# One gathered tile in 72 fetched row by row from SP's queue: a graph layer on one core

## The chip, the core and the metric

The kernel runs on one core of a Trainium2 chip. A core has TensorE (PE in the profile), VectorE (DVE), ScalarE (ACT), GpSimd (POOL) and SyncE (SP), each with its own instruction stream. They meet through semaphores and share 16 DMA engines. SP computes nothing: it waits, loads registers and issues transfers. POOL issues the indirect transfers, whose row addresses come from a list of indices in on-chip memory. The metric is the device time of one execution in microseconds (us).

## What is computed

A message-passing layer on a graph with 12,500 nodes and 412,500 edges, sorted by target node, 96 channels wide. Cut to what matters:

```python
def _mlp(h, W, b, gamma, beta):
    h = relu(h @ W + b)
    mu, var = mean(h, axis=0), mean(square(h - mean(h, axis=0)), axis=0)
    return gamma * (h - mu) * rsqrt(var + 1e-5) + beta

node_feat = _mlp(x, W_node, b_node, g_node, beta_node)
edge_feat = _mlp(edge_attr, W_edge, b_edge, g_edge, beta_edge)
message = concatenate([x[src], x[dst], edge_feat], axis=1)      # 412500 x 288
message = _mlp(message, W_msg, b_msg, g_msg, beta_msg)
agg = segment_sum(message, dst, num_segments=12500)
return layernorm(x + agg + node_feat)
```

The sources `src` are random, so each of the 412,500 edges needs some row of 96 floats (384 bytes).

## The kernel before

**Tables.** The product of x with the source part and with the target part of `W_msg` is made once per node and kept in device memory: `p_tab` for sources, `q_tab` for targets. An edge then needs the row `p_tab[src]`.

**Tiles, groups, blocks.** A tile is 128 edges, one on each partition; there are 3223. Four tiles (`GT`) make a group: 806 groups (`NG`). Four groups (`BG`) make a block: 202 blocks. `gather(g, pg)` (L162) fetches one group into the buffer `pg` with four indirect transfers issued by POOL (L166), one for each tile: 128 rows of 384 bytes each.

**Early and late groups.** The first 104 groups (`SPILL`) are gathered while the tables, the node part and the edge statistics are computed, and are written out to `spill`. All later groups go into a ring of 21 buffers (`RING`): 21 groups are gathered ahead of the main loop (L355), and from then on one more group is asked for, by `ahead_of` (L332), each time the loop has used one late group (L536 to L538). So group `ahead` goes into the buffer that group `ahead - 21` has just left.

**The main loop** (L514 to L538) goes over `steps`, all groups in the order of `order`: 176 late blocks, with the 26 early blocks spread between them. Its order is written out by hand for all five engines (`manual_schedule`): each engine carries out its instructions in program order. At the first group of block number `s`, SP issues `load(s + 2)` and `fetch(s + 1)`. `load` (L390) fetches edge attributes and relative targets for two blocks at a time (L399, L400), loads one register with the block's first node (L403), and copies target rows from `q_tab` into one of three `rhs` buffers (L408); the address comes from that register. That last transfer waits until PE has done its products (L455) with the `rhs` buffer's former contents. `fetch` (L411) brings an early block back from `spill` (L415). PE makes the edge part and adds the target rows (L440, L455), DVE adds the gathered rows (`message`, L466), ACT applies relu (L473), PE sums by target and collects the statistics (L488), DVE adds the sums into `agg` (L501, L502).

**After the loop** the last statistics are made, and the output is normalised and written (L709 to L742).

Transfers issued by SP take eight completion semaphores in turn, and each transfer waits for the one that used its semaphore before, eight transfers back.

Of the kernel before, what the change touches and what calls it, by code (L numbers as in the profile page):

```python
# [11 lines left out]
F32 = mybir.dt.float32  # L12
I32 = mybir.dt.int32
# [3 lines left out]
ET = mybir.EngineType  # L17
# [3 lines left out]
N, C, E, ED = 12500, 96, 412500, 4  # L21
EPS = 1e-5
P = 128
# [3 lines left out]
GT, GE, BG = 4, 512, 4  # L27
NT = -(-E // P)
NG = -(-NT // GT)
NBL = -(-NG // BG)  # L30
NTP, NGP = NBL * BG * GT, NBL * BG
EP = NGP * GE
# [19 lines left out]
SPILL = 26 * BG  # L52
RING = 21
RAW = 3
SKEW = 8
HB, RB = 2, 3
CL, CE = 2, 2
J = 8


# [12 lines left out]
def gnn(ctx, tc, t):  # L73
    nc = tc.nc
    const = ctx.enter_context(tc.tile_pool(name="const", bufs=1))
    dram = ctx.enter_context(tc.tile_pool(name="dram", bufs=1, space=DRAM))
    p_tab = dram.tile([NN, C], F32, name="p_tab")
# [11 lines left out]
    ring = rpool.enter_context(tc.tile_pool(name="ring", bufs=RING))  # L89
# [16 lines left out]
    wide = const.tile([P, P], F32, name="wide")  # L106
# [52 lines left out]
                (nc.scalar if (c // CH + k) % 2 else nc.sync).dma_start(outs[k][:, c:c + CH, :], r[:, :, k, :])  # L159
            yield  # L160

    def gather(g, pg):  # L162
        tab, idx = (t["x"], src_raw) if g < RAW * BG else (p_tab, src)
        for i in range(min(GT, NT - g * GT)):
            k = g * GT + i
            nc.gpsimd.indirect_dma_start(  # L166
                out=pg[:, i, :], out_offset=None, in_=tab[:, :],
                in_offset=bass.IndirectOffsetOnAxis(ap=idx[:, k:k + 1], axis=0))
        return pg
# [107 lines left out]
    def edge_norm():  # L277

        with tc.tile_pool(name="es", bufs=2) as work, tc.tile_pool(name="es1", bufs=1) as one, \
                tc.tile_pool(name="es_ps", bufs=4, space=PSUM) as ps:  # L280
            stats = one.tile([P, NS, NBL, 6], F32, name="estats")
            for b in range(NBL):
                if b % J == 0:
                    yield
                    ea = work.tile([P, J, GE], F32, name="ea")
                    n = min(J, NBL - b)
                    for i in range(NS):
                        nc.sync.dma_start(ea[Q * i:Q * i + 2 * EK, :n, :],
                                          t["ea"][EK * i:EK * (i + 2), b:b + n, :])
                for i in range(NS):  # L290
                    k = NS * b + i
                    if k % 2 == 0:
                        pr = ps.tile([P, 2, GE], F32, name="pr")
                    nc.tensor.matmul(pr[:, k % 2, :], wide[Q * i:Q * i + 2 * EK, :],  # L294
                                     ea[Q * i:Q * i + 2 * EK, b % J, :], start=True, stop=True)
                    if k % 2:
# [32 lines left out]
            nc.vector.tensor_scalar(w_e, w_msg[:, 2, :], a_e, None, op0=OP.mult)  # L329

    def fast(ring):
        def ahead_of(g):  # L332
            return gather(g, ring.tile([P, GT, C], F32, name="pg"))

        with tc.manual_schedule(engines={ET.SP, ET.Pool}):
            nc.sync.dma_start(q_tab[:WM, :], zero[:WM])
# [18 lines left out]
            got = {g: ahead_of(g) for g in range(SPILL, SPILL + RING)}  # L355
# [11 lines left out]
        with tc.tile_pool(name="fix", bufs=1) as fix, tc.tile_pool(name="msg", bufs=2) as work, \  # L367
# [22 lines left out]
            def load(s):  # L390

                b = order[s]
                first = SPILL // BG
                c, o = ((b - first) // CL * CL + first, CL) if b >= first else (b // CE * CE, CE)
                if c not in eas:
                    o = min(o, NBL - c)
                    eas[c] = work.tile([P, o, GE], F32, name="ea" if b >= first else "eae")
                    for i in range(BG):
                        nc.sync.dma_start(eas[c][Q * i:Q * i + EK, :, :], t["ea"][EK * i:EK * (i + 1), c:c + o, :])  # L399
                    nc.sync.dma_start(eas[c][EK:P:Q, :, :], rel_d[:, c * BG * GE:(c + o) * BG * GE]  # L400
                                      .rearrange("o (b g e) -> (o g) b e", g=BG, e=GE))
                ea = eas[c][:, b - c, :]
                _, val = nc.values_load_multi_w_load_instructions(  # L403
                    base[:, b:b + 1], engines=[ET.SP], min_val=0, max_val=N - 1,
                    skip_runtime_bounds_check_because="they are nodes' numbers")
                rows = q_tab[bass.ds(val[0], WN), :]
                rows = bass.AP(rows.tensor, rows.offset, [[C, WN], [WS * C, BG], [1, C]], None, rows.runtime_checks)
                nc.sync.dma_start(rhs[C:C + WN, s % RB, :, :], rows)  # L408
                block[s] = ea

            def fetch(s):  # L411
                b = order[s]
                if b * BG < SPILL:
                    back = work.tile([P, BG, GT, C], F32, name="pb")
                    nc.sync.dma_start(back, spill[b].rearrange("p g (a c) -> p g a c", a=GT))  # L415
                    for i in range(BG):
                        got[b * BG + i] = back[:, i, :, :]
# [18 lines left out]
            def edges(s):  # L436

                prs[s] = ps.tile([P, BG, GE], F32, name="pr", bufs=1)
                for i in range(min(BG, NG - order[s] * BG)):
                    nc.tensor.matmul(prs[s][:C + WN, i, :], we[Q * i:Q * i + EK + 1, :],  # L440
                                     block[s][Q * i:Q * i + EK + 1, :], start=True, stop=True)

            def prepare(s):

                n = min(BG, NG - order[s] * BG)
                pr, x = prs[s], left[s % 2]
                nc.scalar.activation(x[:C, :n, :], pr[:C, :n, :], AF.Relu)  # L447
                nc.vector.tensor_scalar(x[C:C + WN, :n, :], pr[C:C + WN, :n, :], 0.0, None, op0=OP.is_equal)  # L448

            def linear(k):  # L450
                s, g = steps[k]
                n = min(GT, NT - g * GT)
                zs[k] = zb[k % 2][:, :GT * C].rearrange("p (t c) -> p t c", c=C)
                for i in range(n):
                    nc.tensor.matmul(zs[k][:, i, :], left[s % 2][:KR, g % BG, i * P:(i + 1) * P],  # L455
                                     rhs[:KR, s % RB, g % BG, :], start=True, stop=True)

            def message(k):
                s, g = steps[k]
                n = min(GT, NT - g * GT)  # L460
                i = g % BG
                h, z, pg = hb[s % HB], zs.pop(k), got.pop(g)
                if i == 0:
                    four[0] = work.tile([P, BG, GT, C], F32, name="hs")
                hs = four[0]
                nc.vector.tensor_add(hs[:, i, :n, :], z[:, :n, :], pg[:, :n, :])  # L466
                if i == min(2, NG - 1 - (g - i)):
                    b = g - i
                    nc.vector.tensor_tensor(  # L469
                        h[:, :, :, C + 1:C + 1 + WN], rel[:, b:b + BG, :].unsqueeze(3).to_broadcast([P, BG, GT, WN]),  # L470
                        nodes_of.unsqueeze(2).to_broadcast([P, BG, GT, WN]), op=OP.is_equal)
                if i == BG - 1 and n == GT:
                    nc.scalar.activation(h[:, :, :, :C], hs, AF.Relu)  # L473
                elif i == BG - 1 or g == NG - 1:
                    for o in range(i + 1):
                        m = GT if o < i else n
                        nc.scalar.activation(h[:, o, :m, :C], hs[:, o, :m, :], AF.Relu)  # L477
# [13 lines left out]
            def add(s):  # L491
# [9 lines left out]
                    nc.vector.tensor_tensor(to, pa[:, i:n:2, C + 1:C + 1 + WN], to, op=OP.add)  # L501
                nc.vector.tensor_add(gram[:, :n, :], pa[:, :n, :C + 1], gram[:, :n, :])  # L502

            n, ahead = len(steps), SPILL + RING
            with tc.manual_schedule(engines={ET.SP, ET.Pool, ET.PE, ET.DVE, ET.Activation}):
                load(0)
                fetch(0)
                load(1)  # L510
                edges(0)
                prepare(0)
                linear(0)
                for k in range(n + SKEW):  # L514
                    s, g = steps[min(k, n - 1)]
                    if k < n and g % BG == 0:
                        if s + 2 < len(order):
                            load(s + 2)
                        if s + 1 < len(order):
                            fetch(s + 1)  # L520
                    if k + 1 < n:
                        linear(k + 1)
                    if k < n:
                        message(k)
                    if 0 <= k - BG < n:
                        sums(k - BG)
                    if k < n and s + 1 < len(order):
                        if g % BG == 0:
                            edges(s + 1)
                        if g % BG == 2:  # L530
                            prepare(s + 1)
                        if g % BG == 3 and order[s + 1] < RAW:
                            convert(s + 1)
                    if k >= SKEW and (k - SKEW) % BG == 0:
                        add((k - SKEW) // BG)
                    if k < n and g >= SPILL and ahead < NG:  # L536
                        got[ahead] = ahead_of(ahead)
                        ahead += 1  # L538

            d = fix.tile([C, BG, C], F32, name="d")  # L540
            s = fix.tile([C, 3], F32, name="s")
# [9 lines left out]
    def general():  # L551

        with tc.tile_pool(name="gd", bufs=1, space=DRAM) as gd, tc.tile_pool(name="gfix", bufs=1) as fix, \
# [138 lines left out]
            for b in range(NB):  # L692
# [7 lines left out]
                nc.vector.tensor_copy(agg[:, WM + b * P:WM + (b + 1) * P], px)  # L700

    fast(ring)
    rpool.close()
    bad = nc.values_load(flag, min_val=0, max_val=1, skip_runtime_bounds_check_because="a comparison's result")
# [72 lines left out]
```

## Time and profile before

| | |
|---|---|
| median of 3 runs | 4132.85 us (4130.39 to 4133.86) |
| the profiled execution | 4122.78 us, span 4121.1 us |
| granted TensorE clock, mean | 0.748 |
| POOL busy | 3066.6 us (74%) |
| PE busy | 2680.6 us (65%) |
| DVE busy | 1710.1 us (41%) |
| ACT busy | 1032.9 us (25%) |
| packets of the hardware queue q1 | 69888, 8.4% of 16 engines' time |
| packets of the software queue q0 | 103136, 16.3% of 16 engines' time |

Busy time is what an engine spent in instructions, of the span of one profiled execution. Register, branch, semaphore and DMA-issuing instructions are not counted as busy, so SP does not stand in that list; its instructions show in the views by line, in the timeline and among the waits. The indirect transfers count as busy on POOL. In a group's row, the idle time behind the bar is that of the engine just before those instructions.

### The profile page before, as it was taken

The page shows a single profiled execution, that of the slowest core. Times are in us where ns is not written, and L with a number is a line of the kernel's source. Part 1 is how long each engine was busy: PE and PEld are TensorE (multiplying, and loading weights), DVE is VectorE, ACT ScalarE, POOL GpSimd, SP SyncE. Part 2 cuts the span into 40 slices and gives each one's busy share as a digit, 9 for nine tenths or more (in the row PEclk, how much of TensorE's full clock was granted, in tenths as well). Part 3 has the DMA queues.
Part 4 walks back from the last instruction along what each step waited for, and adds up shares of the span by engine and source line. Part 5 has one row for each costly group of instructions (what it writes and reads, how often), then busy time and mean ns, then how long its engine had stood idle before and what let it go on. Part 6 is the DMA issues. An engine that isn't in the chain of part 4 may idle for free. (4 is left out here: it accounts for less than half of the span.)

```text
span 4121.1 us, 46085 instructions
## 1 busy us (share of the span) xinstructions
PE 2680.6 (65%) x16509; PEld 2234.5 (54%) x16509; DVE 1710.1 (41%) x2609; ACT 1032.9 (25%) x800; POOL 3066.6 (74%) x3244
## 2 busy tenths in 40 slices
PE   4699968866566655666665656665666666665666
PEld 4555536755555555555555545554556555554556
DVE  2599984433333332333233333332333333332333
ACT  1377742221112211122111111211121111111121
POOL 6777777777777777777777777777777777777774
PEclk7555557877778877778787777887777778877786
DMA  8555532222221222122212121222212212222123
GB/s 247 159 109 112 106 72 58 55 54 53 53 53 46 53 54 53 46 54 53 52 47 54 52 54 45 54 54 53 54 45 53 53 46 54 54 52 53 46 53 109
DMA packets 188576, 270.79 MB, mean 66 GB/s; under 512 B 121095, under 2 KB 121480, under 8 KB 187330
## 3 DMA queue, kind: packets, MB, share of 16 engines
q0 software_dynamic: 103136, 158.62, 16.3%
q1 hardware_dynamic: 69888, 95.64, 8.4%
q10 hardware_dynamic: 15312, 13.47, 1.2%
q8 instruction: 133, 2.18, 0.2%
q14 instruction: 107, 0.88, 0.1%
HBM read 225.90 MB, written 41.60 MB: 65 GB/s over the span
## 5 line engine op out<-in xcount | busy, mean ns | idle before, releaser
L166 POOL DMA_INDIRECT pg<-p_tab,src x2807 | 2648.5, 944 | 855.5 <-issue 699.4
L455 PE MATMUL z<-rhs,left 128*128 128x96 f32 x6446 | 1104.7, 327 | 1264.1 <-DVE left L448 1081.2
L455 PEld LDWEIGHTS z<-rhs,left 128*128 128x128 f32 x6446 | 998.7, 236 | 1494.1 <-DVE left L448 1129.8
L466 DVE TENSOR_TENSOR hs<-z,pg 128x384 f32<-128x384 f32 x702 | 391.3, 557 | 1996.5 <-DMA pg<-p_tab,src 1830.9
L488 PE MATMUL pa<-h 128*97 128x128 f32 x6446 | 1006.6, 308 | 4.5 <-DVE agg L501 4.1
L488 PEld LDWEIGHTS pa<-h 128*97 128x97 f32 x6446 | 894.5, 194 | 4.9 <-ACT h L477 4.2
L473 ACT ACTIVATE h<-hs 128x1536 f32<-128x1536 f32 x201 | 298.2, 1483 | 1811.9 <-DVE hs L466 1811.9
L447 ACT ACTIVATE left<-pr 96x2048 f32<-96x2048 f32 x202 | 377.4, 1868 | 914.3 <-PE pr L440 914.3
L448 DVE TENSOR_SCALAR left<-pr 31x2048 f32<-31x2048 f32 x202 | 462.9, 2291 | 21.6 <-ACT left L447 15.3
L166 POOL DMA_INDIRECT stage<-p_tab,src x368 | 353.5, 961 | 124.6 <-issue 107.6
L294 PE MATMUL pr<-ea,wide 10*128 10x512 f32 x1212 | 372.2, 1062 | 21.2 <-DMA ea<-in_ea 21.2
L300 DVE BATCH_NORM_STATS2 estats<-r 128x6 f32<-128x512 f32 x606 | 361.4, 680 | 28.9 <-ACT r L298 28.8
L298 ACT ACTIVATE r<-pr 128x1024 f32<-128x1024 f32 x303 | 293.3, 1024 | 144.2 <-PE pr L294 117.5
L294 PEld LDWEIGHTS pr<-ea,wide 10*128 10x128 f32 x1212 | 209.4, 318 | 182.7 <-issue 87.9
L440 PE MATMUL pr<-ea,we 6*127 6x512 f32 x1404 | 203.4, 648 | 12.3 <-DMA ea<-rel_d 12.3
L469 DVE TENSOR_TENSOR h<-rel,z 128x496 f32<-128x496 f32 x202 | 133.2, 660 | 0.0
L501 DVE TENSOR_TENSOR agg<-pa,agg 97x62 f32 x404 | 89.9, 223 | 63.7 <-PE pa L488 49.1
L502 DVE TENSOR_TENSOR gram<-pa,gram 97x388 f32<-97x388 f32 x202 | 111.3, 551 | 0.2
L466 DVE TENSOR_TENSOR hs<-z,pb 128x384 f32<-128x384 f32 x104 | 57.9, 556 | 108.0 <-PE z L455 107.0
L440 PEld LDWEIGHTS pr<-ea,we 6*127 6x127 f32 x1404 | 55.3, 184 | 38.2 <-issue 13.4
L166 POOL DMA_INDIRECT stage<-in_x,src_raw x48 | 45.5, 947 | 25.1 <-issue 11.0
L266 PE MATMUL py<-center,xp 96*128 96x96 f32 x196 | 42.8, 423 | 26.4 <-ACT xp L261 13.4
(108 smaller groups left out, 566.0 us busy)
## 6 DMA issues: line engine op xcount, KB each, us to landing
pg<-p_tab,src POOLq DMA_INDIRECT x2807
spill<-stage SPq DMA_DIRECT2D x26, 768.0 KB
pb<-spill SPq DMA_DIRECT2D x26, 768.0 KB
ea<-in_ea SPq DMA_DIRECT2D x75, 160.0 KB
rhs<-q_tab SPq DMA_DIRECT2D x202, 46.5 KB
ea<-in_ea SPq DMA_DIRECT2D x352, 20.0 KB
stage<-p_tab,src POOLq DMA_INDIRECT x368
y_d<-y0s SPq DMA_DIRECT2D x12, 384.0 KB
```

Source lines behind the costliest of these rows:

```text
L166: nc.gpsimd.indirect_dma_start(out=pg[:, i, :], out_offset=None, in_=tab[:, :], in_offset=bass.IndirectOffsetOnAxis(ap=idx[:, k:k + 1], ax ...
L294: nc.tensor.matmul(pr[:, k % 2, :], wide[Q * i:Q * i + 2 * EK, :], ea[Q * i:Q * i + 2 * EK, b % J, :], start=True, stop=True)
L298: nc.scalar.activation(r, pr, AF.Relu)
L300: nc.vector.bn_stats(stats[:, (k - o) % NS, (k - o) // NS, :], r[:, 1 - o, :])
L440: nc.tensor.matmul(prs[s][:C + WN, i, :], we[Q * i:Q * i + EK + 1, :], block[s][Q * i:Q * i + EK + 1, :], start=True, stop=True)
L447: nc.scalar.activation(x[:C, :n, :], pr[:C, :n, :], AF.Relu)
L448: nc.vector.tensor_scalar(x[C:C + WN, :n, :], pr[C:C + WN, :n, :], 0.0, None, op0=OP.is_equal)
L455: nc.tensor.matmul(zs[k][:, i, :], left[s % 2][:KR, g % BG, i * P:(i + 1) * P], rhs[:KR, s % RB, g % BG, :], start=True, stop=True)
L466: nc.vector.tensor_add(hs[:, i, :n, :], z[:, :n, :], pg[:, :n, :])
L469: nc.vector.tensor_tensor(h[:, :, :, C + 1:C + 1 + WN], rel[:, b:b + BG, :].unsqueeze(3).to_broadcast([P, BG, GT, WN]), nodes_of.unsqueeze ...
L473: nc.scalar.activation(h[:, :, :, :C], hs, AF.Relu)
L488: nc.tensor.matmul(pas[s][:, g % BG, :C + 1 + WN], h[:r, i, :C + 1], h[:r, i, :C + 1 + WN], start=i == 0, stop=i == n - 1)
```

## The change

In the main loop one tile in 72 is no longer gathered by POOL. The loop counts the groups it asks for in runs of 18 (`SG = SS * ceil(128 / SR)` = 2 * 9). Of the first group of such a run, POOL gathers three tiles, and SP fetches the 128 rows of the fourth by 128 transfers of one row each. They are spread over the run: at every second group SP loads 15 row numbers into 15 registers with one instruction, and issues 15 transfers (8 in the last of the nine portions), each with its address from a register. The row numbers come as a line of 128 integers, fetched into the first row of a constant tile that is not used any more by then (`wide`), once for each run. The first portion waits until the buffer's former group has been used. A run is started so only if it is whole, which gives 37 such runs and 4736 rows.

```diff
+SR, SS = 15, 2
+SG = SS * -(-P // SR)
...
-    def gather(g, pg):
+    def gather(g, pg, without=0):
         tab, idx = (t["x"], src_raw) if g < RAW * BG else (p_tab, src)
-        for i in range(min(GT, NT - g * GT)):
+        for i in range(min(GT, NT - g * GT) - without):
...
+            lin = wide[0:1, :].bitcast(I32)
+
+            def row_numbers(g):
+
+                nc.sync.dma_start(lin, t["rows"][g * GT + GT - 1:g * GT + GT, :])
+
+            def rows_of(pg, lo, hi):
+                _, val = nc.values_load_multi_w_load_instructions(
+                    lin[:, lo:hi], engines=[ET.SP], min_val=0, max_val=N - 1,
+                    skip_runtime_bounds_check_because="they are nodes' numbers")
+                for p in range(lo, hi):
+                    nc.sync.dma_start(pg[p:p + 1, GT - 1, :], p_tab[bass.ds(val[p - lo], 1), :])
...
             n, ahead = len(steps), SPILL + RING
+            row_numbers(ahead)
...
                     if k < n and g >= SPILL and ahead < NG:
-                        got[ahead] = ahead_of(ahead)
+                        m = (ahead - SPILL - RING) % SG
+                        if m == 0:
+                            by_row = ahead if ahead + SG <= NG else None
+                        got[ahead] = ahead_of(ahead, int(ahead == by_row))
+                        if by_row is not None and m % SS == 0:
+                            lo = m // SS * SR
+                            rows_of(got[by_row], lo, min(lo + SR, P))
+                            if m == SG - SS and by_row + 2 * SG <= NG:
+                                row_numbers(by_row + SG)
                         ahead += 1
...
+    give("rows", np.pad(s, (0, EP - E)).reshape(NTP, P))
```

`rows` is the list of sources again, laid out one tile to a line; `ahead_of` passes `without` on to `gather`.

More of the change, by code (lines that the diff above doesn't have):

```diff
@@ L331, in fast, with ahead_of @@
     def fast(ring):
-        def ahead_of(g):
-            return gather(g, ring.tile([P, GT, C], F32, name="pg"))
+        def ahead_of(g, without=0):
+            return gather(g, ring.tile([P, GT, C], F32, name="pg"), without)
         with tc.manual_schedule(engines={ET.SP, ET.Pool}):
```

## The prediction

> **What bounds the kernel now.** First the page's costliest groups: which line owns the span?
>
> ```profile
> L166 POOL DMA_INDIRECT pg<-p_tab,src x2807 | 2648.5, 944 | 855.5 <-issue 699.4
> ...
> L466 DVE TENSOR_TENSOR hs<-z,pg 128x384 f32<-128x384 f32 x702 | 391.3, 557 | 1996.5 <-DMA pg<-p_tab,src 1830.9
> ...
> L166 POOL DMA_INDIRECT stage<-p_tab,src x368 | 353.5, 961 | 124.6 <-issue 107.6
> ...
> L166 POOL DMA_INDIRECT stage<-in_x,src_raw x48 | 45.5, 947 | 25.1 <-issue 11.0
> ```
>
> POOL shows as 74% busy, but the pause before each indirect transfer belongs to it. Busy and idle of the three L166 rows together are 3504.0 + 478.1 + 70.6 = 4052.7 us of a span of 4121.1. One gather in the main part takes (2648.5 + 855.5) / 2807 = 1.248 us. Behind it DVE waits 1830.9 us for gathered rows. Second, the timeline of POOL at the end of the loop: is the pause a wait that would grow or vanish?
>
> ```profile
> 4049.69 0.94 POOL L166 DMA_INDIRECT pg<-p_tab,src  x1 [0.30 <-issue]
> 4050.94 0.94 POOL L166 DMA_INDIRECT pg<-p_tab,src  x1 [0.30 <-issue]
> 4052.19 0.94 POOL L166 DMA_INDIRECT pg<-p_tab,src  x1 [0.30 <-issue]
> 4053.44 0.94 POOL L166 DMA_INDIRECT pg<-p_tab,src  x1 [0.31 <-DMA pg<-p_tab,src]
> ```
>
> No: one gather every 1.25 us to the last, and the pause is the same whatever releases it. The rest of the span, about 67 us, follows the last gather. The chain of waits on the page only follows that tail, so it is no guide to the loop.
>
> Third, SP, which is to do the new work: its waits, and its instructions by line.
>
> ```profile
> SPq L408 <- PE z L455: 2860.3, 199, 34.5
> ```
> ```profile
> L403 SPq TENSOR_LOAD <-base x202: 426/530/947, 619.0 to 3986.8; - x101
> ```
> ```profile
> L408 SPq FUSED_REGOPS  x202: 37/37/51, 619.9 to 3987.3; - x101
> L408 SPq MOVE rhs<-q_tab x202: 29/29/39, 620.0 to 3987.5; - x101
> L408 SPq DMA_DIRECT2D rhs<-q_tab x202: 258/289/308, 620.1 to 3999.2; - x101
> ```
> ```profile
> 609.55 7.57 SPq L375 DMA_DIRECT2D rhs<-bias  x12
> ```
>
> SP stands 2860 us at one wait, for `rhs` to come free. The next rows are minimum/median/maximum in ns: a register load, and the three instructions of a transfer with its address from a register, which is the kind added here. The last row gives the gap between two of SP's instructions: 12 transfers whose median, by line, is 588 ns take 7.57 us, so (7.57 - 12 x 0.588) / 11 = 0.047 us each.
>
> **What goes from POOL.** 681 groups are asked for inside the loop; 37 whole runs of 18 fit. 37 gathers x 1.248 = 46.2 us, all of it on the path, since POOL neither waits nor pauses otherwise and the tail hangs on its last gather. What is late next is the consumer: it has 1830.9 us of waiting for rows, so the saved 46 do not meet another engine.
>
> **What comes onto POOL.** A buffer that SP filled is given back to POOL 21 groups later, so the gathers into it get waits on SP's semaphores; the built program has 146 more wait instructions on POOL (989 for 843). They wait for transfers long landed. At 17 ns each (a wait instruction in the L408 view) and a gap of 0.047 they would cost 146 x 0.064 = 9.3 us if nothing covered them. The sequencer runs them while the gather before is still going: the 0.30 pauses are equal with and without a semaphore behind them. I take 0 and keep 9.3 as an end.
>
> **What comes onto SP.** In each run of 18 groups POOL now needs 71 x 1.248 = 88.6 us; SP must fit into that.
> - One row: 0.037 + 0.029 + 0.289 + 3 gaps of 0.047 = 0.50. That transfer has 124 rows; a single row of 384 bytes without a register (L192) took 0.26 in SP's timeline, which gives 0.47. I take 0.47, nearest in shape; ends 0.45 and 0.50. 128 x 0.47 = 60.2 us.
> - One portion's load of 15 registers by a single instruction. The trace has only loads of one, 0.53. Bounds: 0.43 (the shortest) and 15 x 0.53 = 7.95 (each word by itself). The nearest row is the same instruction, one read of neighbouring words; I take its longest, 0.95. 9 x 0.95 = 8.5 us.
> - The old work of 4.5 late blocks: 0.53 + 0.037 + 0.029 + 0.289 + 4 gaps = 1.07 for the target rows, and half of the 2.4 us that one pair's edge transfers fill in the timeline; together 2.27 x 4.5 = 10.2. Early blocks, 26 for 176 late ones, 0.66 for each run: 1.07 + 1.2 + 0.78 (L415) = 3.05, so 2.0. The list of row numbers: 0.3.
>
> Sum 60.2 + 8.5 + 10.2 + 2.0 + 0.3 = 81.2 of 88.6 us: SP is 92% full and 7.4 us are free. The change is covered, but by little. It costs nothing while a row stays under 0.47 + 7.4 / 128 = 0.53, or a portion's load under 0.95 + 7.4 / 9 = 1.77 us, which is (1.77 - 0.53) / 14 = 0.089 us for each further register.
>
> [...]
>
> **Waits that the change adds.** Each row waits for the transfer eight back: 8 x 0.47 = 3.8 us. The last gather's rows reach DVE 1.8 us after POOL is done with it (end 4054.38, next addition 4056.21), so a small transfer is in by then; only behind the 768 KB of an early block, 26 times, may SP stand a few us. The first portion waits for `message` of that very group (DVE, L466). Queued behind it on SP stands the next block's `load`, and behind that PE's L440 and L455 of two blocks on. A block lasts 16 x 1.248 = 20 us and SP works 2 x 8 + 2.3 = 18 in it, so `load` comes some us later than now and still a block early. The last portion is asked for five groups, 25 us, before the group is used.
>
> **The rivals.**
> - SP becomes the bound through the 15-register load (slower). Against it: one instruction, one contiguous read. For it: the trace cannot exclude that each word is read alone, and one word costs DVE's own register load (L495) 0.304. With that for each further word a load is 0.53 + 14 x 0.304 = 4.8, SP needs 116 us where a run took 72 x 1.248 = 89.9 before, and (116 - 89.9) x 37 = 960 us are added. Half of that price, 0.15, gives 2.63, SP 96.4 and (96.4 - 89.9) x 37 = +240: about 4370, which I give for this rival. It decides from 0.089 us a word, and is slower than before from (89.9 - 81.2) / 9 = 0.97 us more a load, which is 0.099 a word. A row could do the same: with the 0.588 of L375, a transfer that the build split in 16 parts, it would cost 0.80, SP 123; but the rows stand unsplit in the built program, like L192.
> - The saving is partly lost: the waits on POOL (9.3), SP standing behind the early blocks, `load` late often enough that PE's edge part holds up POOL through the ring. It needs more than 21 groups of delay to reach POOL, or a late last portion each time. Between the two ends: 4098 to 4133.
> - A gather is not worth 1.248, because POOL's pause is paid once for a group. Against it: the pauses are equal within a group, and the rate is the same to the end.
>
> **How the numbers follow.** The profiled execution is 4122.78 us, 1.7 above its span, and 10.1 below the median of the runs. 4122.8 - 46.2 = 4076.6 there, and 4132.9 - 46.2 = 4086.7 in the median: 4087. The main case's own range is 4082 to 4098 (the 9.3 us upward, the spread of the runs downward), chance 0.64. Partial loss, 4098 to 4133: 0.06. SP just over its limit, 4133 to 4200: 0.10. Far over: 0.20. The range 4080 to 4200 leaves out the last. About 0.2% (8 us) is what a measurement here can tell from no change: faster 0.64 + 0.04 = 0.68, same 0.04, slower 0.28.
>
> **What would show it.** Right: L166 with 2770 `pg` transfers, still 0.94 and 0.30 each; in SP's views 4736 row transfers near 0.26 to 0.29, a load of 15 registers under 1.8 us, and SP still standing at L408 for PE, some 7.4 x 37 = 270 us in all; DVE still waiting mostly for gathered rows. Wrong: a load of 15 registers of 2 us or more, no wait left on SP at L408, POOL with new pauses released by DVE (the ring not free), and DVE waiting at the 37 row-fetched groups for a transfer of SP's. If the pauses on POOL grow without that, the waits on its own queue cost what I left out.

## The result, and the profile after

| | before | after |
|---|---|---|
| median | 4132.2 us (4130.39 to 4133.86, 4 runs) | 4229.55 us (4226.04 to 4240.41, 4 runs) |
| profiled execution, span | 4122.78, 4121.1 us | 4240.41, 4238.6 us |
| granted TensorE clock, mean | 0.748 | 0.718 |

The ratio is 1.0242 [1.0229, 1.0254]: 97 us slower, where 46 us faster were predicted. Measured a second time (`after_again`, below), it was 1.0242 [1.0222, 1.0263]. All lines below are those of the changed kernel, where L166 has become L168, L403 L405, L408 L410, L415 L417, L440 L442, L455 L457 and L466 L468. L510 fetches the list of row numbers, L513 loads registers from it, L517 issues the rows.

First the groups of the page, POOL's gathers and the two engines behind them:

```profile
L168 POOL DMA_INDIRECT pg<-p_tab,src x2770 | 2619.9, 946 | 977.0 <-issue 726.7
...
L442 PE MATMUL pr<-ea,we 6*127 6x512 f32 x1404 | 259.0, 812 | 534.3 <-DMA ea<-rel_d 533.4
...
L468 DVE TENSOR_TENSOR hs<-z,pg 128x384 f32<-128x384 f32 x702 | 389.0, 557 | 1617.8 <-PE z L457 1125.9
```

The 37 gathers are gone, as the change says (2770 for 2807). But busy and idle of POOL's row come to 2619.9 + 977.0 = 3596.9 us for 3504.0: 92.9 us more, where 46.2 less were expected. The usual pause of 0.305 us for 2770 gathers would be 844 us of idle time; 977.0 are 133 more, and the gathers themselves are 6 us longer (946 ns each for 944). DVE no longer waits mostly for gathered rows; it waits for PE, and PE for edge attributes and relative targets (`ea`) that SP fetches.

Next SP's instructions by line (minimum/median/maximum in ns), the new ones:

```profile
L513 SPq TENSOR_LOAD <-wide x333: 742/3291/3489, 630.8 to 4078.9; - x167
```
```profile
L517 SPq FUSED_REGOPS  x4736: 37/37/42, 632.4 to 4083.4; - x198
L517 SPq MOVE pg<-p_tab x4736: 29/29/38, 632.7 to 4083.5; - x198
L517 SPq DMA_DIRECT2D pg<-p_tab x4736: 217/225/1797, 633.3 to 4083.5; - x198
```

A row is cheaper than was taken (a transfer of 225 ns for 289). A load of 15 registers has a median of 3.29 us, where 0.95 was taken and 1.77 was named as the most that SP could bear. Is SP full, then? Its waits between 1900 and 3800 us answer that, before the change and after it (total us, times, longest):

```profile
SPq L408 <- PE z L455: 1634.0, 110, 20.2
```
```profile
SPq L513 <- DMA wide<-in_rows: 15.2, 10, 1.6
SPq L517 <- DMA rhs<-q_tab: 2.6, 8, 0.5
SPq L410 <- PE z L457: 0.3, 1, 0.3
```

Of these 1900 us SP stood 1634 at one wait before, and some 18 in all after. SP sets the pace of the loop now. The waits of the other engines show who is held up by it:

```profile
PE pr L442 <- DMA ea<-rel_d: 533.4, 59, 15.2
DVE hs L468 <- DMA pb<-spill: 497.2, 22, 33.5
...
PE z L457 <- DMA rhs<-q_tab: 349.8, 54, 11.9
...
DVE hs L468 <- DMA pg<-p_tab,src: 169.7, 23, 19.0
POOL pg L168 <- DVE hs L468: 156.9, 86, 14.5
DVE hs L468 <- DMA wide<-in_rows: 155.6, 10, 20.7
...
DVE hs L468 <- DMA pg<-p_tab: 74.8, 7, 20.5
```

Everything that SP issues comes late: its old transfers (edge attributes with relative targets, early blocks, target rows) and the new rows. The new rows do not stand under one name here. A wait for several transfers is listed under the one that came last; DVE itself reads nothing of the list in `wide`. But all ten waits for `wide<-in_rows` and all seven for `pg<-p_tab` fall on groups that SP has filled in part. Taken group by group from the trace, DVE waits 408 us in all at the 37 row-fetched groups (59 at the same groups in the kernel before). At 29 of them it waits more than a microsecond, and begins 1.1 to 2.3 us after SP's last row instruction. One of these places, SP first and then DVE:

```profile
2594.65 3.38 SPq L517 DMA_DIRECT2D pg<-p_tab  x8
2598.12 0.23 SPq L510 DMA_DIRECT2D wide<-in_rows  x1
```
```profile
2600.11 1.02 DVE L468 TENSOR_TENSOR hs<-z,pg 128x384 f32<-128x384 f32 x2 [20.73 <-DMA wide<-in_rows]
```

And one with an early block:

```profile
2180.98 15.88 SPq L517 DMA_DIRECT2D pg<-p_tab  x30
...
2200.25 0.78 SPq L417 DMA_DIRECT2D pb<-spill  x1
```
```profile
2206.85 0.56 DVE L468 TENSOR_TENSOR hs<-z,pb 128x384 f32<-128x384 f32 x1 [31.13 <-DMA pb<-spill]
```

An early block is asked for only after 30 rows and the load between them, 15.9 us, and DVE has stood 31 us when it arrives. From DVE the delay reaches POOL through the ring: POOL's wait in the list above, 156.9 us, up to 14.5 at a time, is for the buffer that DVE has not yet left.

**Why one load is long and another not.** The nine portions of a run start at bytes 0, 60, 120, ... 480 of the list, and SP's loads fall into three kinds. These are portions 0, 1, 2, 4 and 8 of one run, by line in a narrow window each:

```profile
L513 SPq TENSOR_LOAD <-wide x1: 1545/1545/1545, 2046.6 to 2046.6; - x1
...
L513 SPq TENSOR_LOAD <-wide x1: 3249/3249/3249, 2056.9 to 2056.9; - x1
...
L513 SPq TENSOR_LOAD <-wide x1: 3362/3362/3362, 2066.5 to 2066.5; - x1
...
L513 SPq TENSOR_LOAD <-wide x1: 1634/1634/1634, 2090.4 to 2090.4; - x1
...
L513 SPq TENSOR_LOAD <-wide x1: 802/802/802, 2131.7 to 2131.7; - x1
```

Portions 0 and 4 start at bytes 0 and 240, multiples of 16, and cost 1.55 to 1.63 us; portion 8 (8 numbers, byte 480) 0.80. All others cost 3.3, portions 2 and 6 among them, which start at multiples of 8 (bytes 120 and 360). The medians of the nine are 1.55, 3.32, 3.31, 3.32, 1.63, 3.32, 3.30, 3.32 and 0.79: 23.8 us for each run of 18 groups.

**The sum with these numbers.** One portion of rows in SP's timeline:

```profile
2151.51 6.01 SPq L517 DMA_DIRECT2D pg<-p_tab  x15
```

From one transfer to the next are (6.01 - 0.225) / 14 = 0.41 us, 52.5 for 128. 52.5 + 23.8 + 0.3 + the old 12.2 = 88.8 us, for 88.6 that POOL needs: full. SP in fact takes 92.6 us for a run: that is the mean distance between the first loads of one run and the next over 20 runs in the middle of the loop (1584 to 3435 us), where SP waits 18 us in all. The same stretch shows what the sum lacks when each instruction is counted with the pause before it: the rows take 54.7 us, the loads 25.0 (23.9 and 1.1 of pauses before them, most of it the wait for the list), the old work 12.6 and the list 0.3. POOL's row gives nearly the same, (3596.9 - 143 x 1.248) / 37 = 92.4, with 143 of the 2770 gathers outside the runs. Against 72 x 1.248 = 89.9 before, SP's 92.6 make 37 x 2.7 = 100 us of loss, for the 97 measured.

Of the 117.5 us by which the two spans differ, 92.9 are POOL's main row; 5.7 are a longer drain at the very end (below); the remaining 19 lie ahead of the first gather and between the last one and the drain, where the consumers finish later than POOL. The granted clock is lower as well (0.718 here, 0.710 in `e_odd`, 0.733 in `e_aligned`, 0.747 in `e_const`, all below). It is TensorE's clock: POOL's gathers, which set the pace where SP does not, stay at 943 to 946 ns throughout, and SP's instructions alone fill the 92.6 us.

### The profile page after: what moved, and what is told of

It reads as the page before. It is cut to its first block, busy times and chain, and to the rows that moved or that the text cites. A ratio compares the mean times of both kernels' runs of the same rounds, so it can differ in the third digit from the quotient of the medians.

```text
span 4238.6 us, 61081 instructions
## 1 busy us (share of the span) xinstructions
PE 2698.1 (64%) x16509; PEld 2222.6 (52%) x16509; DVE 1699.0 (40%) x2609; ACT 1032.2 (24%) x800; POOL 3040.1 (72%) x3207
## 5 line engine op out<-in xcount | busy, mean ns | idle before, releaser
L168 POOL DMA_INDIRECT pg<-p_tab,src x2770 | 2619.9, 946 | 977.0 <-issue 726.7
L457 PE MATMUL z<-rhs,left 128*128 128x96 f32 x6446 | 1077.8, 322 | 731.4 <-DMA rhs<-q_tab 349.8
L457 PEld LDWEIGHTS z<-rhs,left 128*128 128x128 f32 x6446 | 989.6, 235 | 975.4 <-issue 535.3
L468 DVE TENSOR_TENSOR hs<-z,pg 128x384 f32<-128x384 f32 x702 | 389.0, 557 | 1617.8 <-PE z L457 1125.9
L490 PE MATMUL pa<-h 128*97 128x128 f32 x6446 | 997.9, 306 | 0.4 <-ACT h L475 0.4
L490 PEld LDWEIGHTS pa<-h 128*97 128x97 f32 x6446 | 886.3, 193 | 0.6 <-ACT h L475 0.6
L442 PE MATMUL pr<-ea,we 6*127 6x512 f32 x1404 | 259.0, 812 | 534.3 <-DMA ea<-rel_d 533.4
L168 POOL DMA_INDIRECT stage<-p_tab,src x368 | 355.6, 966 | 125.7 <-issue 109.3
L442 PEld LDWEIGHTS pr<-ea,we 6*127 6x127 f32 x1404 | 69.0, 226 | 563.7 <-issue 547.4
L468 DVE TENSOR_TENSOR hs<-z,pb 128x384 f32<-128x384 f32 x104 | 57.7, 555 | 530.0 <-DMA pb<-spill 497.2
L503 DVE TENSOR_TENSOR agg<-pa,agg 97x62 f32 x404 | 89.9, 223 | 91.1 <-PE pa L490 82.6
L442 PE MATMUL pr<-eae,we 6*127 6x512 f32 x208 | 40.1, 849 | 73.7 <-DMA eae<-rel_d 73.7
L168 POOL DMA_INDIRECT stage<-in_x,src_raw x48 | 45.6, 949 | 25.8 <-issue 11.3
```

What stands on the lines that cost most here:

```text
L168: nc.gpsimd.indirect_dma_start(out=pg[:, i, :], out_offset=None, in_=tab[:, :], in_offset=bass.IndirectOffsetOnAxis(ap=idx[:, k:k + 1], ax ...
L490: nc.tensor.matmul(pas[s][:, g % BG, :C + 1 + WN], h[:r, i, :C + 1], h[:r, i, :C + 1 + WN], start=i == 0, stop=i == n - 1)
```

## The experiments

Theory A: SP's time is full, and what fills it is the register loads. Rivals: B, thousands of small transfers hold up the queue, or each other. C, it is the place in SP's order: the first portion's wait for `message`, and the old loads that stand behind rows, cost some us for each run whatever a load takes. D, long loads on SP do harm by themselves. Six of the twelve runs, `e_half` to `e_half4`, `e_few` and `e_few2`, were on four chips where the kernel before itself took 5285 to 5374 us; they are compared with that alone.

**1. `e_aligned`: the same numbers, each portion at a multiple of 64 bytes** (two lines of the tile instead of one; the same 333 loads and 4736 rows).

```diff
-            lin = wide[0:1, :].bitcast(I32)
+            lin = wide[0:2, :].bitcast(I32)
...
-                    lin[:, lo:hi], engines=[ET.SP], min_val=0, max_val=N - 1,
+                    lin[lo // 120:lo // 120 + 1, lo // SR % 8 * 16 + 0:lo // SR % 8 * 16 + 0 + hi - lo], engines=[ET.SP], min_val=0, max_val=N - 1,
...
+    r = np.zeros((NTP, 2 * P), np.int32)
+    for i in range(0, P, SR):
+        r[:, i // SR * 16 + 0:i // SR * 16 + 0 + min(SR, P - i)] = np.pad(s, (0, EP - E)).reshape(NTP, P)[:, i:i + SR]
```

> Same runs, rows and transfers as the changed kernel; only the place of the row numbers differs, so that every load of 15 starts on a 64-byte boundary. In the changed kernel's trace the loads that start on a 16-byte boundary took 1.55 to 1.63 us and the six others of a run 3.3 us. Theory A (SP's time is full, and the register loads fill it): loads 1.6, so SP needs 52.5 for rows + 8 x 1.6 + 0.8 + 0.3 + 12 of old work = 78 of 88.6 us in a run; POOL no longer stalls, and the time is 4132 - 46 + 8 for the slightly longer gathers = about 4094 (4085 to 4105). Theory B (the 4736 small transfers hold up the others in the queue, the loads are a side matter): loads shorter, time still 4200 or more. Theory C (the place in SP's order and the wait for the buffer's former group cost some 4 us a run, however full SP is): 4200 or more as well.

Measured: 4082.91 us (4081.53 to 4084.01), 0.9904 [0.9888, 0.9921] of the kernel before on that chip: 39.4 us faster instead of 97 slower, by nothing but where the numbers lie. By line, and from the waits and groups:

```profile
L513 SPq TENSOR_LOAD <-wide x333: 744/1602/1817, 626.5 to 3829.0; - x167
```
```profile
SPq L410 <- PE z L457: 212.5, 36, 19.8
```
```profile
L168 POOL DMA_INDIRECT pg<-p_tab,src x2770 | 2613.6, 944 | 844.7 <-issue 661.4
```

All loads are short now, SP has 212.5 us to stand again, and POOL's row is 3458.3 us, 45.7 less than before: 37 gathers of 1.248 us, 46.2. POOL's longer drain takes 5.7 back, which leaves 40.5. The expected range began at 4085: it was reckoned from 4132 for the kernel before, which took 4122 here, and with 8 us for longer gathers, which did not come (944 ns). This sets A apart from B and C: rows, waits and order are those of the changed kernel.

SP is full here too, for a while. From 1000 to 1820 us it waits 1.1 us at L410, and a run takes it 82.7 us. That is less than POOL's 88.6, so POOL is not held up. At the first 14 row-fetched groups DVE still stands up to 17.4 us; from the eighteenth on the last row is asked for 16 us or more before it is used. SP has caught up by then, and its waits at L410 return.

**2. `e_odd`: the same, each portion 4 bytes behind a multiple of 64** (`* 16 + 1` for `* 16 + 0` above and in the list).

> As the aligned one, but every portion's numbers start 4 bytes behind a 64-byte boundary. Theory A: eight loads of 3.3 and one of about 1.9 us, 28.4 us a run in place of 23.8 in the changed kernel; SP is the bound, so 4.6 x 37 = 170 us more: about 4400 (4350 to 4420). Theory B and C: as the changed kernel, 4215 to 4245.

Measured: 4373.91 us (4371.31 to 4376.52), 1.061 [1.0589, 1.0631].

```profile
L513 SPq TENSOR_LOAD <-wide x333: 1876/3293/3547, 628.0 to 4214.9; - x167
```
```profile
POOL pg L168 <- DVE hs L468: 300.3, 83, 21.6
```

Between this kernel and `e_aligned` lie 291 us and four bytes. Over the changed kernel it is (1.061 - 1.0242) x 4122.35 = 152 us; by A, eight loads of 3.29 and one of 1.88 make 28.2 us for a run where there were 23.8, and 37 x 4.4 = 163. By the distance between first loads a run takes SP 96.5 us (20 runs from 1616 to 3546 us), 3.9 more than in the change. The eight numbers of the last portion show the price too: 1.91 for 0.78 in the median.

**3. `e_const`: no loads, the rows' addresses are constants** (128 fixed rows of the table, so the rows are not those that the edges name).

```diff
-                _, val = nc.values_load_multi_w_load_instructions(
...
-                    nc.sync.dma_start(pg[p:p + 1, GT - 1, :], p_tab[bass.ds(val[p - lo], 1), :])
+                    nc.sync.dma_start(pg[p:p + 1, GT - 1, :], p_tab[97 * p:97 * p + 1, :])
```

> The 128 rows of a run are fetched by 128 transfers with constant addresses, so the rows are not those of the edges; the register loads and the address instructions are left out, the transfers, their order and their waits stay. Theory A: a row costs SP 0.23 + 0.05 = 0.28 us, a run 36 + 0.3 + 12 = 48 of 88.6 us: 4085 to 4100. Theory B: the transfers are all there and come faster, so 4220 or more. Theory C: the order and the first portion's wait are all there: above 4180.

Measured: 4083.71 us (4083.46 to 4083.96), 0.9906 [0.9886, 0.9926].

```profile
L514 SPq DMA_DIRECT2D pg<-p_tab x4736: 211/247/1386, 629.0 to 3822.0; - x198
```
```profile
SPq L410 <- PE z L457: 774.9, 101, 19.5
```

4736 small transfers, the first portion's wait and SP's order are all there, and nothing is lost: B and C fall. SP has 774.9 us to spare, and still the kernel is no faster than `e_aligned`, where it has 212.5: beyond the point where SP is covered, POOL decides.

**4. `e_16`: sixteen rows at a time, one tile in 64** (`SR, SS = 16, 2`). A run is 16 groups, 42 runs fit, and a portion starts at a multiple of 64 bytes without more ado.

> 16 rows at a time in place of 15: one tile in 64, 42 runs, and every load starts on a 64-byte boundary by itself. Theory A: a load of 16 takes 0.3 + 4 x 0.24 = about 1.3 us, SP needs 52.5 + 8 x 1.3 + 0.3 + 10.7 = 74 of 63 x 1.248 = 78.6 us, and 42 x 1.248 = 52.4 us are saved less 8 for longer gathers: about 4088, faster than before although SP gets more rows for its time. Theory B and C: more runs, so more loss than in the changed kernel: 42 x 3.6 = 150 lost, 52 saved, about 4230 to 4260.

Measured: 4076.21 us (4073.94 to 4081.91), 0.9886 [0.9869, 0.9902].

```profile
L513 SPq TENSOR_LOAD <-wide x336: 1132/1218/1416, 631.8 to 3874.2; - x168
```
```profile
SPq L410 <- PE z L457: 85.2, 13, 16.5
```
```profile
L168 POOL DMA_INDIRECT pg<-p_tab,src x2765 | 2608.8, 943 | 843.7 <-issue 666.5
```

42 gathers of 1.248 are 52.4 us; less 5.3 for the drain (9.65 us here) 47.1, and 46.1 were measured. Sixteen registers are loaded faster than fifteen: 1.22 for 1.60. The 1.3 expected for it was the author's estimate. By the sum SP needs 52.5 + 8 x 1.22 + 0.3 + 10.8 = 73.4 of a run's 63 x 1.248 = 78.6 us; by the distance between first loads it takes 76.7 (20 runs from 1429 to 2963 us, with 0.3 us of waiting at L410 for `z`). Its wait at L410 over the whole loop is down to 85.2 us: POOL is just not held up. The expected 4088 had 8 us for longer gathers in it, which did not come (943 ns), and began from a slower kernel before. This version beats both kernels.

**5. `e_16_again` and `after_again`**, both kernels once more, side by side on one chip.

> 16 rows at a time once more. Theory A, where the kernel before takes about 4125 us: 46 us less, as measured. Where it takes 5300 us: 42 runs of 128 + 12 + 12 = 152 us are 6390, about 7300 in all (6800 to 7600): SP was full to 97% on the first chip, so whatever makes its instructions dearer goes straight into the time. A theory in which SP's time does not set the pace gives a ratio of 0.99 in both cases.

> The changed kernel itself, beside the next one on the same chip. Theory A, where the kernel before takes about 4125 us: some 100 us more, as measured. Where it takes 5300 us, as in the three runs of one tile in 144: a row cost SP about 1.0 us there, in place of 0.41, so a run would need 128 + 29 + 14 = 171 us, 37 runs 6330, and with some 900 us ahead of and behind the loop about 7200 (6800 to 7500). A theory in which SP's time does not set the pace gives the same ratio of 1.02 in both cases.

Measured: `e_16_again` 4078.09 us (4075.07 to 4079.03), 0.9889 [0.9872, 0.9905]; `after_again` 4223.29 us, 1.0242 [1.0222, 1.0263]. The second profiled execution of the changed kernel has POOL's row at 944 ns a gather, for 946 in the first, and nearly the same waits:

```profile
L168 POOL DMA_INDIRECT pg<-p_tab,src x2770 | 2613.6, 944 | 968.7 <-issue 670.5
```
```profile
POOL pg L168 <- DVE hs L468: 150.3, 87, 10.1
```

The row is 2613.6 + 968.7 = 3582.3 us, 78.3 above the kernel before, for 92.9 in the first: the slower of the two executions is the one taken apart above, and the loss does not hang on that.

**6. `e_few`: all loads as in the change, but one transfer of 15 neighbouring rows for each portion** (starting at the first number's row; 14 of 15 rows are not the edges').

```diff
-                for p in range(lo, hi):
-                    nc.sync.dma_start(pg[p:p + 1, GT - 1, :], p_tab[bass.ds(val[p - lo], 1), :])
+                nc.sync.dma_start(pg[lo:hi, GT - 1, :], p_tab[bass.ds(val[0], hi - lo), :])
```

> All loads of 15 as in the changed kernel, but each portion is fetched by one transfer of 15 neighbouring rows from the first number's row on, so 14 of 15 rows are not those of the edges; 333 transfers in place of 4736. Theory A: SP needs 23.8 for loads + 9 x 0.45 + 0.3 + 12 = 40 of 88.6 us: as the one with constant addresses, 4080 to 4090. Theory D (the long register loads hurt by themselves, by holding up what stands behind them): still well above 4122.

> The kernel of e_few once more, on another chip, for the same reason. Theory A: SP needs 40 of 88.6 us in a run; 46.2 us saved less 6 for the end: some 40 us less than the kernel before on the same chip. Theory D (the long register loads hurt by themselves): slower than before.

Measured: 5318.7 for 5351.81 us, 0.9936 [0.9915, 0.9957], and 5330.19 for 5362.84, 0.9941 [0.9919, 0.9963].

```profile
L513 SPq TENSOR_LOAD <-wide x333: 53/3277/3409, 991.2 to 5089.9; - x167
```

The loads are as long as in the change, and the kernel is faster by 33 us: long loads do no harm where SP has the time for them. That speaks against D, with a reserve. It was seen only where the kernel before takes 5350 us, and there POOL does not set the pace alone: in `e_few` it waits 906.7 us for DVE to leave a buffer, where on a usual chip the kernel before has no pause over 0.4 us between these gathers. What leaves D no room in the changed kernel is the accounting above, where SP's own instructions and pauses fill the 92.6 us.

**7. `e_half`: every second run only, one tile in 144** (19 runs).

```diff
-                            by_row = ahead if ahead + SG <= NG else None
+                            by_row = ahead if ahead + SG <= NG and (ahead - SPILL - RING) % (2 * SG) == 0 else None
...
-                            if m == SG - SS and by_row + 2 * SG <= NG:
-                                row_numbers(by_row + SG)
+                            if m == SG - SS and by_row + 3 * SG <= NG:
+                                row_numbers(by_row + 2 * SG)
```

> The changed kernel with only every second run of 18 groups fetching rows: one tile in 144, 19 runs, unaligned loads as in the changed kernel. Theory A (SP's time in sum): a run overfills SP by some 4 us, the next 18 groups leave SP nearly idle and the lag is made up before it reaches POOL through the 21 groups of the ring; POOL does not stall and 19 x 1.248 = 23.7 us are saved, less some 6 us that the end has grown in every kernel of this kind: 4122 - 24 + 6 = 4104 (4098 to 4110). Theory C (each run costs its 4 us where it stands): 19 x 4 = 76 lost, about 4175.

> The kernel of e_half once more, on another chip, since there the kernel before itself took 5352 us. Theory A (SP's time in sum): a run overfills SP by some 4 us, the next 18 groups leave it nearly idle; 23.7 us saved, 6 us for the longer end: about 18 us less than the kernel before on the same chip (12 to 24 less). Theory C (each run costs its 4 us where it stands): 19 x 4 = 76 lost, some 50 us more than before.

> The kernel of e_half a third time, since the kernel before took 5363 us on the second chip too. Theory A (SP's time in sum): about 18 us less than the kernel before on the same chip (12 to 24 less), no stalls of POOL. Theory C (each run costs its 4 us where it stands): some 50 us more than before, with a stall of POOL of 4 us in each of the 19 runs.

> One tile in 144 a fourth time, for a chip on which the kernel before takes about 4125 us. Theory A (SP's time in sum): some 18 us less than before (12 to 24 less), POOL without stalls. Theory C (each run costs its 4 us where it stands): some 50 us more than before, POOL with a stall of 4 us in each of the 19 runs.

Measured: 1.0712 [1.069, 1.0735], 1.0717 [1.0692, 1.0743], 1.0674 [1.0624, 1.0724] and 1.0722 [1.0699, 1.0744]: all four 6.7 to 7.2% slower than the kernel before beside them, where A expected faster and C 1.2% slower. But on these chips SP itself is slower. In `e_half`, by line and in the timeline:

```profile
L517 SPq FUSED_REGOPS  x2432: 2/37/1407, 994.3 to 5580.8; - x188
```
```profile
2080.73 38.07 SPq L517 DMA_DIRECT2D pg<-p_tab  x30
```

An instruction of 37 ns takes up to 1.4 us here, and 30 rows with the load between them 38 us, for the 15.9 above. SP is not alone in it: before the weight loads of the sums (L490) PE's loading side idles 536.5 us for which the profile shows nothing that it waited for; in the changed kernel it idles 0.6 us there in all. No theory's number applies. The changed kernel with all its runs was not measured on such a chip, so half the rows cannot be set against all of them, and what half the runs would give on a chip of the usual kind stays open.

## Why the prediction was wrong

**The step that failed** is the portion's load: "I take its longest, 0.95. 9 x 0.95 = 8.5 us". It measured 23.8 / 9 = 2.64 us in the mean, 3.3 in six of nine portions, so 15.3 us more for a run: with it a run takes SP 92.6 us, where 81.2 were added up and POOL needs 88.6. Moving the numbers alone (`e_aligned`, `e_odd`) shows that this term decides. The price of a register was bounded rightly, from 0.43 to 7.95 for the load, but the value was taken at the end where the words cost next to nothing, because the nearest row was "the same instruction, one read of neighbouring words". A row of a load of one word says nothing of the price of further words; the only row that bore on that was DVE's 0.304 for a word by itself, and it was left to a rival.

**The limit that was named** lay between two prices: 0.089 us for each further register. With 0.53 for one word (L403 in the kernel before) SP's loads show (3.3 - 0.53) / 14 = 0.198 us for a portion that starts off a 16-byte boundary (the change, `e_odd`) and (1.60 - 0.53) / 14 = 0.076 for one that starts on it (`e_aligned`). The same instruction lies on either side of the limit by the place of its words alone, and six of nine portions lay on the dear side.

**The row** was taken at 0.47, a little above its lower end of 0.45; it was 0.41 within a portion, and with all pauses the rows took 54.7 us a run. That gave back 60.2 - 54.7 = 5.5 us a run, which was luck: nothing in the profile before told it. At the price taken the kernel would have lost an estimated 37 x 5.5 = 204 us more.

**The sum of SP** was of the right kind. What SP takes for a run, measured, against what POOL needs, separates the kernels that lose from those that win: 92.6 and 96.5 us of 88.6 lose (the change, `e_odd`), 82.7 of 88.6 and 76.7 of 78.6 win (`e_aligned`, `e_16`). Sums from medians, 88.8, 78.5 and 73.4, are 3 to 4 us short each time, because they leave out the rows that take longer than the median (2.2 us in the change), the pauses before the loads (1.1) and some of the old work (0.4). With the measured times the free time agrees too: (88.6 - 82.7) x 37 = 218 us in `e_aligned`, of which 212.5 were seen at L410, and (78.6 - 76.7) x 42 = 80 in `e_16`, where 85.2 were.

**"`load` comes some us later than now and still a block early"** was wrong with the loads as they are: in the 20 us of a block SP had not 18 us of work but up to 2 x (15 x 0.41 + 3.3) + 2.3 = 21.2, and 92.6 / 4.5 = 20.6 in the mean. So the blocks came later and later until POOL stood still for them. Hence the waits at L442, L457 and L468 above. "The last portion is asked for five groups, 25 us, before the group is used" failed in the same way: in 29 of 37 runs DVE already stood waiting for it. The four signs of being wrong that were named at the end all came: a load of 2 us or more, next to no wait at L410 (71.6 us for 2860.3 at L408, and 0.3 in the middle of the loop), POOL released by DVE, and DVE waiting at the row-fetched groups.

**Right** were the value of a gather (1.248 us, `e_aligned`), nothing for POOL's 146 added waits (its pauses are 0.3 us in `e_aligned` too), the reserve of the consumer, and the form of the limit, that the change costs nothing while a load stays short enough: at 1.60 us (`e_aligned`) it cost nothing, at 2.64 (the change) it did. The figure in it, 1.77, was not tested, since no run on a usual chip lies between those two. With what SP's other work measured it would be (88.6 - (92.6 - 23.9)) / 9 = 2.2 us, an estimate. The reason given for the waits holds for a part of them only: of the 680 on POOL's queue after 650 us in the kernel before, 218 fall under the gather before and 462 into the pause behind it, which is 0.305 us in the median with a wait in it and without.

**The rivals.** The first, SP bound through the load, is what happened; it was given less weight than the main case. By its point a load had to cost 0.97 us more than taken, 1.92 in all, for the kernel to be slower than before; that lies between the 1.60 of `e_aligned` and the 2.64 of the change. Its 4370 was built on a load of 2.63, within 0.01 of the mean, and on a run of 96.4 us. The closeness of the load is luck: 2.63 came from half of DVE's price for a word, and no single load costs that, but 3.3, 1.6 or 0.8. The run measured 92.6, because the rows took 5.5 us less and the pauses before loads and the old work some 1.5 more: 37 x (92.6 - 89.9) = 100 us lost instead of 240. The partial loss and the cheaper gather did not happen.

## What to carry to other kernels

When an idle engine is given work in small pieces, add up its whole time for one period of the engine that sets the pace, and look for the term whose size no row of the trace shows: if the sum stands at 92%, that term decides, and it is worth measuring by itself before the rest. Where a load of many numbers into SP's registers starts is worth a measurement: 15 numbers took 1.6 us from a 16-byte boundary of the list and 3.3 off it, and that alone was the difference between 2.4% slower and 1.0% faster; with sixteen numbers for fifteen, in 1.22 us, it was 1.1%. Such an engine may be full and cost nothing, as long as its whole time for a period is below that of the engine that sets the pace (76.7 of 78.6 us in `e_16`). Above it, everything that it issues comes late, the old requests queued behind the new work as much as the new work itself; and a wait view may list that delay under several names.

## What the runs showed of the hardware that was not expected

- SP's load of several registers from on-chip memory by where it starts in the list: 15 words 3.3 us off a 16-byte boundary (8-byte boundaries included), 1.55 to 1.63 on it; 16 words on it 1.22; 8 words on it 0.78 in the median, 4 bytes behind it 1.91. So 15 words on the boundary take longer than 16, and the 15 of `e_odd` cost 3.3 although they hold three whole 16-byte pieces too. An estimate that fits these times is 0.3 us and, on the boundary, 0.24 for each four words and 0.20 for each word left over (0.78 for 8, 1.62 for 15, 1.26 for 16), off it 0.20 for every word (1.9 for 8, 3.3 for 15). What SP does within a load was not shown.
- POOL's drain at the end of the program, before and after the change (minimum/median/maximum ns of three):

```profile
L773 POOLq DRAIN  x3: 40/113/4365, 4115.8 to 4120.8; - x3
```
```profile
L798 POOLq DRAIN  x3: 40/113/10037, 4227.4 to 4238.0; - x3
```

In these runs the long one goes with the number of gathers in the program, not with SP's rows: 4.37 us with 2807, 2.87 with 2788 (`e_half`), 10.04 with 2770 (10.06 in `e_few`, with 333 transfers of SP's for 4736), 9.65 with 2765. From 2765 to 2770 it is 0.39 us longer and from 2788 to 2807 1.50, both times 0.08 us for each gather; from 2770 to 2788 it is 7.2 us shorter. So 5.7 us of what the change cost seem to hang on how many gathers remain; no number between 2770 and 2788 was tried.
- Chips on which the kernel before takes 5285 to 5374 us, and on which SP's 37-ns instructions now and then take a microsecond. They are exactly the four chips on which `e_half` ran; whether the chip is the cause, or something that went with these runs, was not separated.
